# A two-layer recurrent kernel on one core: VectorE's weight work placed behind the first normalization, loads reordered, and a rearranged last block

## The chip, the cores and the metric

The kernel runs on one core of one Trainium2 chip. The core has five engines that run side by side, each with its own in-order queue: TensorE (PE in the profile, its weight loads PEld), VectorE (DVE), ScalarE (ACT), GpSimd (POOL) and SyncE (SP), which here only issues DMAs. The metric is device time of one execution in microseconds; lower is better.

## The reference

The input x has 4 sequences of 1024 tokens with 128 features. Two layers run over it. Each computes `x = x + s * g`, with xn the normalized x, s a sequence mixer and g the SiLU of a feed-forward network.

```python
x = L0_attn_x
xn = _layernorm(x)
s = _L0_attn_ref(xn, ...)        # q k^T with decay GAMMA**(i-j), times v
g = _silu(_L0_ffn_ref(xn, ...))  # silu(xn w1)*(xn w2), gelu(h1), gelu(h2), w3; width 512
x = x + s * g
xn = _layernorm(x)
s = _L1_attn_ref(xn, ...)        # W_in, causal conv of 4 taps, SiLU, state scan, SiLU gate, W_out
g = _silu(_L1_ffn_ref(xn, ...))  # top half of the tokens by router score through W1, GELU, W2
x = x + s * g
```

The state scan of the second layer keeps 16 states for each of the 128 features: `h = A*h + x_conv*B`, with `A = exp(-exp(A_log))`, and `y = sum(C*h) + D_param*x_conv`. The router takes the 512 highest of 1024 scores in each sequence.

## The kernel before

The 4096 tokens are cut into 8 blocks of 512 (NBK, HB); blocks 2b and 2b+1 are the halves of sequence b. Features lie on the 128 partitions, the 512 tokens of a block along the free dimension; x itself lies with tokens on partitions, in 4 chunks of 128 (CB).

**The order of the work** is not that of the text. Every helper (mm, act, copy, vcopy, vtt, stt, ptt, dma) only records an operation with an engine and an estimated cost. `Plan.order` then plays all recorded operations through a list scheduler: an operation has a due time (prio), an operation with an earlier due time goes first among those that are ready, and its ready time follows from the estimated costs, a model of the DMA ring, the free buffers of each pool tag, and 1.28 us for a change of ScalarE's table. That charge is made for SiLU, GELU and the tanh GELU only: `act` passes no table kind for Exp. `Plan.issue` emits the operations in that order (L373), each engine's order fixed by hand-made dependencies, so L373 is the line of nearly every instruction in the profile. Due times come from `TIMES`: for each stage a length and eight starts, one for each block, spread over the stage's operations by `Plan.spread`. An operation's `late` set holds others that must be planned before it without a semaphore between them.

**Start** (L508 to L649). All loads go on SP: x of block 0, vec, one table of constants cs (ident, mask, tie, sel, rowdec, coldec), wqk, A_log, the weights w12, wv, h1, h2 (in four row chunks each), w3 and so on, and x of blocks 1 to 4. VectorE rounds weights to the fp32r type by copies (w12_t, h_t, wgh, ...), some split in a high and a low part (M, wg, wcv, W1, wr). ScalarE computes logA by two Exp activations; VectorE copies it and tie into a PSUM bank, bankA. rep, four 128x128 selections of ident, is copied by VectorE too.

**Per block j**: `ln0` and `ln1` normalize by `layernorm`: bn_stats and bn_aggr on VectorE, ve = variance + eps (VectorE), rs = ve to the power -0.5 (GpSimd), tm = -mean*rs (VectorE), xn = x*rs + tm (ScalarE), four transposes tr (TensorE), then copies xh, xl. `retention` is the first mixer (pq, pv, psc, pz, po). `gated`, `hidden1`, `hidden2`, `out0` are the first feed-forward network: p and a; pa, ga, g_h and g_l; pb and h; pg. The parts g_h come from ScalarE, g_l from GpSimd. `front` is the convolution (px, xc) and stores xc to DRAM as xd. `states` makes B and C, `gates` the gate (pt), `router` the scores (pr), `moe` the second feed-forward network (pm, hm, pmo, ff), `ranks` the ranking (cmp, eq, rank, wm), `scans` the state scan, `project` W_out (y, pyo, so), and `finish` the gating and the store.

`scans` works through 8 tiles u of 128x2x512: DMA xd into u (broadcast to 16 states), u*B (VectorE), two scans along time (VectorE), u*C (GpSimd; the very last on VectorE), then sums over states into py (TensorE). There are 6 u buffers. In the last block the first two u tiles come from TensorE through rep (pu) instead of a DMA (U_BY_PE).

Of the kernel before, what the change touches and what calls it, by code (L numbers as in the profile page):

```python
# [8 lines left out]
FR = mybir.dt.float32r  # L9
# [4 lines left out]
P = 128  # L14
NB, L, D = 4, 1024, 128
NCH = L // P
HB = 512
# [30 lines left out]
for _name, _w in (  # L48
    ("ident", P), ("mask", P), ("tie", P), ("sel", P), ("rowdec", 1), ("coldec", 1),
):  # L50
    _CST[_name] = (_n, _n + _w)
    _n += _w
NCST = _n
# [7 lines left out]
    "ln0": (10.465, (-34.463, 37.568, 0.307, -8.702, 29.140, 25.837, -0.706, 2.276)),  # L61
    "retention": (7.697, (19.747, 29.540, 0.054, 5.261, 0.588, -0.481, 27.669, 17.510)),
    "gated": (0.198, (17.080, -12.778, -2.899, 37.127, 52.075, 3.684, 35.848, 24.681)),
    "hidden1": (181979.521, (10.669, -0.997, 0.654, 26.140, 49.753, 13.692, 29.323, 21.440)),
    "hidden2": (104.604, (6.706, 7.824, 35.607, 17.363, 7.255, 8.335, 12.787, 23.305)),
    "out0": (0.269, (-10.144, 10.621, 13.685, 32.888, 37.354, 6.208, 14.587, 34.725)),
    "ln1": (0.086, (-3.447, -9.822, 3.389, 39.108, 24.646, 10.527, 7.924, 19.641)),
    "front": (99775.310, (31.104, -7.375, 49.241, 35.721, 3.625, 15.911, 8.435, 28.268)),
    "states": (1929558528.870, (-22.925, -12.719, -2.927, -2.692, -1.385, 5.843, 8.364, 33.960)),
    "gates": (2802.502, (-10.124, -3.354, -1.683, 3.017, 7.752, 67.130, 11.212, 9.313)),  # L70
    "router": (35.459, (32.003, 36.047, 1.039, 23.096, 29.397, 12.314, 55.205, 9.245)),
    "moe": (0.850, (-6.037, 10.367, -2.942, 3.023, 8.714, 12.982, 45.904, 32.432)),
    "ranks": (3.658, (7.924, -5.386, 32.363, 0.750, 18.387, 5.771, 15.184, 9.739)),
    "scans": (0.083, (26.879, 6.452, 3.058, 25.041, 26.277, 9.568, 13.774, 14.948)),
    "project": (0.218, (-2.585, 1.221, 6.521, 8.046, 9.527, 12.283, 10.650, 21.658)),
    "finish": (2311.973, (10.042, -1.800, 14.285, 18.479, 29.156, 18.433, 18.474, 24.699)),
    "load_x": (0.107, (32.705, -1.570, 6.609, 55.729, 2.835, 7.712, 33.265, 51.716)),
}
SWITCH = 0.725
SPARE = 2  # L80
XB = 5
# [300 lines left out]
def tile_kernel(  # L382
# [34 lines left out]
    for name, n in {  # L417
        "x": XB, "stat0": 2, "ve0": 2, "rs0": 2, "tm0": 2, "stat1": 2, "ve1": 2, "rs1": 2, "tm1": 2, "col": 2, "wm": 2, "most": 2, "eq": 2,
        "nxt": 2, "xn0": 2, "xnT": 1, "qT": 1, "vd": 1, "sT": 1, "st": 1, "y": 1,
        "sc": 1, "xh0": 2, "xl0": 2, "sO": 2, "xh1": 2, "xl1": 2, "Br": 1, "Cr": 2, "bc": 1,  # L420
        "gate": 2, "xc": 2, "cmp": 2, "a": 3, "xn1": 3, "ff": 3, "so": 3,
        "hh": 8, "hl": 8, "h2": 5, "u": 6, "last": 2,
    }.items():
        early = name in ("a", "h2")
        plan.tag(sb, name, n, early or name in ("hh", "hl", "u"), 1 if early else None)
# [17 lines left out]
    def mm(o, lhsT, rhs, start, stop):  # L443
        n = rhs.length()
        one = rhs.root.dtype != F32
        cost = (n + 38) / 2400 if one else 4 * max(n / 2400, 0.0536)
        if o.shape[0] < P:
            cost += 0.12
        do("tensor", "matmul", o, lhsT=lhsT, rhs=rhs, start=start, stop=stop, cost=cost)
# [62 lines left out]
    cs = load("cs", cst, (P, NCST))  # L512
    wqk_s = load("wqk_s", wqkT, (P, 2 * D), "sT")

# [3 lines left out]
    wv_t = load("wv_t", wv, (P, D))  # L518
    sel = load("sel", by_state(cst[:, slice(*_CST["sel"])]), (P, P))
# [28 lines left out]
    def c(name):  # L548
        a, b = _CST[name]
        return cs[:, a:b]  # L550
# [5 lines left out]
    ident = c("ident")  # L556
# [34 lines left out]
    w12_t = tile_("const", "w12_t", (P, 2 * F), FR)  # L591
# [3 lines left out]
    for i, s in enumerate(h_s):  # L595
        h_t.append([tile_("const", f"h{i}_t{k}", (P, F), FR) for k in range(KC)])
        for k in range(KC):
            vcopy(h_t[i][k], s[k])
# [6 lines left out]

    rep_t = tile_("const", "rep", (P, 4 * P))
    rep = [rep_t[:, i * P : (i + 1) * P] for i in range(4)]
    for i in range(4):
        vcopy(rep[i].split(NS), c("ident")[:, 4 * i * E : (4 * i + 1) * E].repeat(NS))
    vcopy(A, logA)  # L610
    vcopy(tie, c("tie"))
# [30 lines left out]
    def add_bias(dst, i):  # L642

        mm(dst, two, bias[:, i * D : (i + 1) * D].repeat(CB), False, True)
# [4 lines left out]
    wr = split(wr_s, "wr", (P, P))  # L649

    def layernorm(j, u, tag):
# [14 lines left out]
        stt(tm, mv[:, :, 0], -1.0, rs, ALU.mult, ALU.mult)  # L666
        xn = tile_(tag, f"xn_{u}", (P, CB, D))
# [144 lines left out]
    def front(j):  # L812

        b, g = divmod(j, NH)
        px = mm_tile(f"px_{j}")
        terms = []
        for k in range(4):
            hi, lo = (t[:, k : k + HB] for t in R[j]["parts"])
            terms += three_pass(wcv, (hi, lo), slice(k * D, (k + 1) * D))
        passes(px, terms)  # L820
        if not g:
            vtt(px[:, 0:3], px[:, 0:3], edges, ALU.subtract)
        xc, xd = tile_("xc", f"xc_{j}"), tile_("xd", f"xd_{j}")
        act(AF.Silu, xc, px, bias=cbias)
        dma(xd, xc)
        R[j].update(xc=xc, xd=xd)

    def states(j):
        xc = R[j]["xc"]
        if j in BY_PE:  # L830
            Bp, Cr = tile_("B", f"B_{j}"), tile_("Cr", f"Cr_{j}")
            mm(Bp, wB, xc, True, True)
            if j in U_BY_PE:
                R[j]["Br"] = Br = tile_("Br", f"Br_{j}")
                act(AF.Identity, Br, Bp, bias=bB)
            act(AF.Identity, Bp, Bp, bias=bB)
# [84 lines left out]
    def scans(j):  # L921
# [7 lines left out]
        for m in range(4):  # L929
            us = []  # L930
            for q in range(0, 4, 2):
                ks = [4 * q + m, 4 * (q + 1) + m]
                u = tile_("u", f"u_{j}_{ks[0]}", (P, 2, HB))
                if m == 0 and j in U_BY_PE:
                    for i, k in enumerate(ks):
                        pu = mm_tile(f"pu_{j}_{k}")
                        mm(pu, rep[q + i], xc, True, True)
                        vtt(u[:, i, :], pu, R[j]["Br"], ALU.mult)
                else:
                    for i, k in enumerate(ks):  # L940
                        dma(u[:, i, :], xd[k * E : (k + 1) * E, :].whole(NS), 0.63, 2.24e5)
                    vtt(u, u, Bp.repeat(2), ALU.mult)
# [15 lines left out]
    def project(j):  # L958
        py = R[j]["py"]
        y = tile_("y", f"y_{j}")  # L960
        stt(py, R[j]["xc"], v("Dp"), py, ALU.mult, ALU.add)
        vtt(y, py, R[j]["gate"], ALU.mult)
        po = mm_tile(f"pyo_{j}", (P, CB, D))
        with fused("tensor", 1.15):
            for i, t in enumerate(chunk):
                mm(po[:, i, :], y[:, t], wout_t, i == 0, False)
            add_bias(po, 0)
        R[j]["so"] = so = tile_("so", f"so_{j}", (P, CB, D))
        copy(so.flat(), po.flat())

    def finish(j):
# [7 lines left out]
        tt = vtt if j == NBK - 1 else ptt  # L979
        tt(so, so, ff, ALU.mult)  # L980
        tt(xg, xg, so, ALU.add)
        dma(out[b, g * HB : (g + 1) * HB, :].rearrange("(c p) d -> p c d", p=P), xg)
# [6 lines left out]
    for j in range(NBK):  # L989
        b, g = divmod(j, NH)  # L990
        for f in (ln0, retention, gated, hidden1, hidden2, out0, ln1, front, states, gates, router, moe, scans, project):
            stage(f, j, j)
        if g == NH - 1:
# [93 lines left out]
```

## Time and profile before

| | |
|---|---|
| median of 3 runs | 418.02 us (417.58 to 420.35) |
| the profiled execution, all | 417.93 us |
| its span, first to last instruction | 416.2 us |
| granted TensorE clock, mean | 0.978 |
| instructions | 6589 |
| ScalarE table loads | 39, 1283 ns each, 50.0 us |
| u multiplied by C on GpSimd | 63, 2389 ns each, 149.7 us |
| u multiplied by B on VectorE | 62, 1206 ns each, 73.5 us |
| scans on VectorE | 128, 1207 and 1266 ns each, 153.3 us |
| loads of u | 124 DMAs of 256 KB, 4.6 us from issue to landing |

Times inside the execution count from the start of the span. A row of the profile in order of time gives start, busy time, engine, line, operation, output <- input with shapes, and in brackets how long the engine had been idle before and what ended that. Busy times of neighbouring rows can overlap a little, since an instruction starts before the one in front has written its last element; the distance from start to start is what a queue pays.

### The profile page before, as it was taken

What the parts mean: (1) busy time and instruction counts of PE and PEld (TensorE: products, weight loads), DVE (VectorE), ACT (ScalarE), POOL (GpSimd) and SP (SyncE); (2) the same over time, 40 slices, a digit from 0 to 9 for tenths busy, and PEclk for the clock granted to TensorE, in tenths of its full rate; (3) what the DMA queues carried; (4) which work ended last, traced back from release to release, by engine and by line L of the source; (5) the groups of instructions that cost most, each with busy time, mean ns of one, the idle gap of its engine ahead of it and who ended that gap; (6) DMA issues with size and microseconds to landing.
All of it is one profiled execution on the core that took longest, in us unless ns stands there. A gap on an engine that the chain in (4) does not pass through costs nothing.

```text
span 416.2 us, 6589 instructions
## 1 busy us (share of the span) xinstructions
PE 389.7 (94%) x2294; PEld 291.1 (70%) x2294; DVE 354.4 (85%) x621; ACT 276.3 (66%) x487; POOL 288.1 (69%) x200
## 2 busy tenths in 40 slices
PE   1999999999999999999999999999999999989843
PEld 1878878866777778777687688677877687747501
DVE  5594605996999968989999969999999999999992
ACT  3687895876557857875867598668577656772600
POOL 3066542198486897869996488967788898773890
PEclk9999999999999999999999999999999999998966
DMA  6900009206418053573602490456073553517300
GB/s 214 330 30 1 2 25 248 57 10 156 120 51 255 27 158 102 133 199 105 202 3 54 132 252 2 116 165 160 1 228 101 158 127 104 125 56 198 103 25 25
DMA packets 37897, 47.44 MB, mean 114 GB/s; under 512 B 7844, under 2 KB 17700, under 8 KB 37864
## 3 DMA queue, kind: packets, MB, share of 16 engines
q1 hardware_dynamic: 37864, 47.02, 40.8%
q8 instruction: 18, 0.29, 0.3%
q14 instruction: 15, 0.12, 0.1%
HBM read 42.40 MB, written 4.60 MB: 113 GB/s over the span
## 4 chain that ended last, share of the span: by engine, by line
PE 82%; DVE 5%; ACT 5%; POOL 4%; issue 2%; DMA 1%; POOLq 1%; SPq 1%; DVEq 0%; ACTq 0%
PE pb L373 15%; PE pa L373 12%; PE p L373 7%; PE py L373 7%; PE pg L373 6%; PE px L373 5%; PE pmo L373 5%; PE pm L373 4%; DVE u L373 4%; PE po L373 3%; POOL u L373 3%; PE pyo L373 2%; PE pv L373 2%; PE psc L373 2%; PE tr L373 2%
## 5 line engine op out<-in xcount | busy, mean ns | idle before, releaser
L373 POOL TENSOR_TENSOR u<-u,Cr 128x1024 f32<-128x1024 f32 x63 | 149.7, 2389 | 31.1 <-ACT last L373 13.0
L373 DVE TENSOR_TENSOR u<-u,B 128x1024 f32<-128x1024 f32 x62 | 73.5, 1206 | 17.1 <-DMA u<-xd 8.7
L373 DVE TENSOR_TENSOR_SCAN u<-bankA,last,u 128x512 f32<-128x512 f32 x64 | 78.5, 1266 | 0.2
L373 DVE TENSOR_TENSOR_SCAN u<-bankA,u 128x512 f32<-128x512 f32 x64 | 74.8, 1207 | 0.4
L373 POOL TENSOR_TENSOR h_l<-a,h_h 128x512 fp32r<-128x512 f32 x32 | 40.9, 1293 | 26.6 <-ACT h_h L373 26.6
L373 ACT ACT_TABLE_LOAD x39 | 50.0, 1283 | 13.6 <-PE pg L373 5.8
L373 POOL TENSOR_TENSOR g_l<-ga,g_h 128x512 fp32r<-128x512 f32 x32 | 40.6, 1293 | 20.5 <-ACT g_h L373 20.5
L373 PE MATMUL pa<-h_h,h_t 128*128 128x512 f32 x128 | 49.6, 405 | 0.0
L373 PE MATMUL pa<-h_l,h_t 128*128 128x512 f32 x128 | 48.6, 397 | 0.0
L373 PE MATMUL pb<-g_h,h_t 128*128 128x512 f32 x128 | 47.3, 396 | 0.0
L373 PE MATMUL pb<-g_l,h_t 128*128 128x512 f32 x128 | 47.1, 395 | 0.1
L373 PE MATMUL py<-u,sel 128*32 128x512 f32 x256 | 40.0, 633 | 7.2 <-POOL u L373 7.2
L373 ACT ACTIVATE h<-pb,vec 128x512 f32<-128x512 f32 x32 | 20.6, 688 | 18.1 <-PE pb L373 16.4
L373 PEld LDWEIGHTS pmo<-W_t,hm 128*128 128x128 f32 x256 | 31.1, 192 | 1.9 <-ACT ff L373 0.8
L373 PE MATMUL pmo<-W_t,hm 128*128 128x128 f32 x256 | 31.5, 275 | 0.0
L373 PEld LDWEIGHTS pg<-w_t,h 128*128 128x128 f32 x256 | 29.9, 192 | 1.0 <-ACT h L373 0.3
L373 PE MATMUL pg<-w_t,h 128*128 128x128 f32 x256 | 30.1, 275 | 0.1
L373 ACT ACTIVATE xn<-x,tm,rs 128x128 f32<-128x128 f32 x64 | 26.9, 486 | 4.6 <-DVE tm L373 4.6
L373 PEld LDWEIGHTS pa<-h_h,h_t 128*128 128x128 f32 x128 | 23.9, 188 | 7.5 <-issue 1.1
L373 PEld LDWEIGHTS pb<-g_h,h_t 128*128 128x128 f32 x128 | 23.9, 188 | 7.0 <-ACT g_h L373 1.3
L373 PEld LDWEIGHTS pa<-h_l,h_t 128*128 128x128 f32 x128 | 24.1, 188 | 6.4 <-POOL u L373 0.8
L373 PEld LDWEIGHTS pb<-g_l,h_t 128*128 128x128 f32 x128 | 23.9, 188 | 6.6 <-POOL g_l L373 1.4
(170 smaller groups left out, 838.3 us busy)
## 6 DMA issues: line engine op xcount, KB each, us to landing
u<-xd SPq DMA_DIRECT2D x124, 256.0 KB, 4.6
x<-in_x_dram SPq DMA_DIRECT2D x8, 256.0 KB, 2.9
xd<-xc SPq DMA_DIRECT2D x8, 256.0 KB, 2.0
out_dram<-x SPq DMA_DIRECT2D x8, 256.0 KB, 3.6
Br<-bd SPq DMA_DIRECT2D x6, 256.0 KB, 4.3
Cr<-bd SPq DMA_DIRECT2D x6, 256.0 KB, 5.6
h_s<-in_h1T_dram SPq DMA_DIRECT2D x4, 256.0 KB, 5.5
h_s<-in_h2T_dram SPq DMA_DIRECT2D x4, 256.0 KB, 4.2
```

Source lines behind the costliest of these rows:

```text
L373: i = getattr(getattr(self.nc, eng), method)(*map(real, args), **{k: real(a) for k, a in kw.items()})
```

## The change

- `layernorm`: when the first one (block 0) has recorded tm, all VectorE operations on weights recorded between `setup = len(plan.ops)` and the definition of `layernorm` get tm in their `late` set, so they are planned behind it. The copies of logA and tie into bankA are recorded after block 0's `ln0`, due at 0.5.
- Loads: ident has a tile and a load of its own, straight after wqk; cs is only mask, rowdec and coldec, and comes behind wv; tie is loaded by itself into the bc buffer. TIMES holds new values, and `mm`'s cost for fp32r is 44 instead of 38 columns over its length.
- `LAST_U`: in the last block the u tiles at index 2 (of 8) take the buffer of w12_t and those at 3 to 6 the four buffers of the hidden weights h_t, which are now laid out in pairs of row chunks (tags w12 and hw); the others take u buffers.
- rep is made in `states` of the last block, by four ScalarE copies into the xnT buffer.
- `project` and `finish` of the last block work in two halves of 256 tokens: py, y, the product with W_out and the last multiplication and addition, and two stores. so*ff reads the product from PSUM, without ScalarE's copy. In all blocks the bias product goes first into pyo instead of last.
- In `front`, the tiles xc and xd are created earlier in the text.

```diff
-    ("ident", P), ("mask", P), ("tie", P), ("sel", P), ("rowdec", 1), ("coldec", 1),
+    ("ident", P), ("mask", P), ("rowdec", 1), ("coldec", 1), ("tie", P), ("sel", P),
...
-NCST = _n
+NCST = _CST["tie"][0]
...
+LAST_U = ("u", "u", "w12", "hw", "hw", "hw", "hw", "u")
...
-        "hh": 8, "hl": 8, "h2": 5, "u": 6, "last": 2,
+        "hh": 8, "hl": 8, "h2": 5, "u": 6, "last": 2, "w12": 1, "hw": 4,
...
-        cost = (n + 38) / 2400 if one else 4 * max(n / 2400, 0.0536)
+        cost = (n + 44) / 2400 if one else 4 * max(n / 2400, 0.0536)
...
-    cs = load("cs", cst, (P, NCST))
     wqk_s = load("wqk_s", wqkT, (P, 2 * D), "sT")
+    ident = load("ident", cst[:, slice(*_CST["ident"])], (P, P))
...
     wv_t = load("wv_t", wv, (P, D))
+    cs = load("cs", cst[:, P:NCST], (P, NCST - P))
+    tie_s = load("tie_s", cst[:, slice(*_CST["tie"])], (P, P), "bc")
...
+    setup = len(plan.ops)
-    w12_t = tile_("const", "w12_t", (P, 2 * F), FR)
+    w12_t = tile_("w12", "w12_t", (P, 2 * F), FR)
...
-        h_t.append([tile_("const", f"h{i}_t{k}", (P, F), FR) for k in range(KC)])
+        pairs = [tile_("hw", f"h{i}_t{k}", (P, 2, F), FR) for k in range(KC // 2)]
+        h_t.append([pairs[k // 2][:, k % 2, :] for k in range(KC)])
...
-    for i in range(4):
-        vcopy(rep[i].split(NS), c("ident")[:, 4 * i * E : (4 * i + 1) * E].repeat(NS))
-    vcopy(A, logA)
-    vcopy(tie, c("tie"))
...
+    setup = [o for o in plan.ops[setup:] if o.eng == "vector"]
...
         stt(tm, mv[:, :, 0], -1.0, rs, ALU.mult, ALU.mult)
+        for o in setup:
+            o.late.add(plan.ops[-1])
+        setup.clear()
...
+                rep = tile_("xnT", "rep", (P, 4, P))
+                R[j]["rep"] = rep = [rep[:, i, :] for i in range(4)]
+                for i in range(4):
+                    copy(rep[i].split(NS), ident[:, 4 * i * E : (4 * i + 1) * E].repeat(NS))
...
-                u = tile_("u", f"u_{j}_{ks[0]}", (P, 2, HB))
+                home = LAST_U[2 * m + q // 2] if j == NBK - 1 else "u"
+                u = tile_(home, f"u_{j}_{ks[0]}", (P, 2, HB))
...
+        n = CB // 2 if j == NBK - 1 else CB
+        R[j]["po"] = po = [mm_tile(f"pyo_{j}_{h}", (P, n, D)) for h in range(0, CB, n)]
+        for h, p in zip(range(0, CB, n), po):
+            t = slice(h * P, (h + n) * P)
+            stt(py[:, t], R[j]["xc"][:, t], v("Dp"), py[:, t], ALU.mult, ALU.add)
+            vtt(y[:, t], py[:, t], R[j]["gate"][:, t], ALU.mult)
+            with fused("tensor", 0.23 * (n + 1)):
+                add_bias(p, 0, True)
+                for i in range(n):
+                    mm(p[:, i, :], y[:, chunk[h + i]], wout_t, False, i == n - 1)
...
+            for h in range(0, CB, CB // 2):
+                t = slice(h, h + CB // 2)
+                vtt(so[:, t, :], R[j]["po"][2 * h // CB], ff[:, t, :], ALU.mult)
+                vtt(xg[:, t, :], xg[:, t, :], so[:, t, :], ALU.add)
+                dma(to[:, t, :], xg[:, t, :])
...
+            if j == 0 and f is ln0:
+                place(0.5)
+                vcopy(A, logA)
+                vcopy(tie, tie_s)
```

## The prediction

> **What bounds the kernel now.** First the busy shares and the 40 slices: which engine is full, and where.
>
> ```profile
> PE 389.7 (94%) x2294; PEld 291.1 (70%) x2294; DVE 354.4 (85%) x621; ACT 276.3 (66%) x487; POOL 288.1 (69%) x200
> ...
> PE   1999999999999999999999999999999999989843
> ...
> DVE  5594605996999968989999969999999999999992
> ```
>
> TensorE is full in every slice but the first and the last ones; nearly all of its 26.5 us of idle time lies at the two ends. The table of equal stretches (columns: length, TensorE, its weight loads, VectorE, ScalarE, GpSimd, clock, DMA) says the same. Most rows give TensorE 25.8 to 26.00 of 26; the ends do not:
>
> ```profile
> 0.00:26.00 26.00, 16.72 (x80) 13.47 (x81) 16.51 (x68) 14.44 (x26) 9.46 (x19) 1.00 0.73 229
> ...
> 364.00:390.00 26.00, 24.42 (x154) 16.18 (x151) 25.17 (x45) 16.38 (x27) 14.18 (x9) 0.93 0.40 103
> 390.00:416.00 26.00, 12.00 (x47) 3.43 (x45) 18.57 (x18) 3.22 (x8) 14.72 (x8) 0.71 0.22 61
> ```
>
> So a gain at the head moves all that follows, a stall put into the middle is paid in full, and the end belongs to VectorE. TensorE's waits between 26 and 366 us are 0.68, 0.23 and 0.19: 1.1 us in all.
>
> Head, in order of time: block 0's normalization is ve (VectorE), rs (GpSimd), tm (VectorE), xn (ScalarE).
>
> ```profile
> 6.55 0.35 DVE L373 TENSOR_SCALAR wqk<-wqk_s,th 128x256 f32<-128x256 f32 x1 [0.41 <-DMA wqk_s<-in_wqkT_dram]
> 6.82 0.15 DVE L373 TENSOR_SCALAR ve<-bankA 128x4 f32<-128x4 f32 x1
> ...
> 8.66 0.15 DVE L373 SCALAR_TENSOR_TENSOR tm<-bankA,rs 128x4 f32<-128x4 f32 x1
> ...
> 8.85 1.65 ACT L373 ACTIVATE xn<-x,tm,rs 128x128 f32<-128x128 f32 x4 [2.89 <-DVE tm L373]
> ```
>
> ve stands behind wqk, whose load was issued fifth, at 3.02; tm comes half a microsecond after rs ended (8.16), behind weight work.
>
> ScalarE in block 0's hidden layers, the place that I count on most below:
>
> ```profile
> 26.69 1.28 ACT L373 ACT_TABLE_LOAD   x1 [1.04 <-PE pa L373]
> 27.98 1.27 ACT L373 ACTIVATE ga<-pa,vec 128x512 f32<-128x512 f32 x2
> ...
> 30.17 0.70 ACT L373 ACTIVATE ga<-pa,vec 128x512 f32<-128x512 f32 x1
> 30.91 0.59 ACT L373 CAST xh<-tr 128x512 fp32r<-128x512 f32 x1
> 31.39 0.62 ACT L373 CAST g_h<-ga 128x512 fp32r<-128x512 f32 x1
> 31.91 0.70 ACT L373 ACTIVATE ga<-pa,vec 128x512 f32<-128x512 f32 x1
> ...
> 35.63 1.85 ACT L373 ACTIVATE h<-pb,vec 128x512 f32<-128x512 f32 x3 [2.03 <-PE pb L373]
> ```
>
> The first h (36.2) is ready only 1.7 us before TensorE wants it: pg starts at 37.93 and ends at 41.42.
>
> The end:
>
> ```profile
> 404.62 1.23 DVE L373 TENSOR_TENSOR u<-u,Cr 128x1024 f32<-128x1024 f32 x1
> 407.87 0.75 DVE L373 SCALAR_TENSOR_TENSOR py<-xc,vec,py 128x512 f32<-128x512 f32 x1 [2.03 <-PE py L373]
> 408.65 0.69 DVE L373 TENSOR_TENSOR y<-py,gate 128x512 f32<-128x512 f32 x1
> 411.45 0.69 DVE L373 TENSOR_TENSOR so<-so,ff 128x512 f32<-128x512 f32 x1 [2.10 <-ACT so L373]
> 412.18 0.69 DVE L373 TENSOR_TENSOR x<-x,so 128x512 f32<-128x512 f32 x1
> ```
>
> From 383.5 to 405.8 VectorE has no gap: it waits for no u transfer there.
>
> The sum is made in this execution's own times: 416.2 us of span, 417.93 us in all, 1.7 us outside the span; the median of the runs, 418.02, is 0.1 higher.
>
> **1. Head.** In the built queue of the changed kernel SP issues x, vec, wqk_s, ident, w12_s. Issues are about 0.5 us apart, so vec goes at 1.22, in A_log's old slot, and wqk at 1.70. A_log (issued 1.22, used at 4.13) took 2.9 us, wqk took 3.5: vec lands near 4.1, wqk at 4.6 to 5.2. VectorE: statistics from 3.58 (0.79), th at about 4.6, ScalarE's exp 0.2 to 5.0, four aggregations of 0.16, wqk 5.2 to 5.55, last aggregation, ve at 5.7. Then 0.15 for ve, 0.16 to GpSimd, 1.03 for rs, 0.13 back: tm at 7.1 with only Mh and Ml in front, against 8.66: **-1.55** (bounds -0.9, if wqk lands 0.6 later than the slower row, and -1.9). The weight work now held behind tm (w12, edge, wr, two, h1) is some 3.5 us before xl at 11.2; xl was at 12.18, so it gains only 1.0, but its first reader stood 1.4 us after its end (12.87 to 14.29), which covers the missing half. The casts themselves are as many; VectorE then idled 3.37 us at 16.90, which takes the rest. cs lands behind wv, needed only by vd (14.67). sel, bB, bC, wout go last and are used from 60 us on. ident by itself adds one issue, tie one more, about 0.5 us each on SP, whose 29 loads ended near 18 us; the next SP work waits for xc, after 60 us. The four rep copies (0.13 from start to start) leave VectorE and become four ScalarE copies in block 7's xnT, between xn and xh; ScalarE's small copies take 0.2 and a 128x128 one 0.41, so 0.8 to 1.6 us, on an engine 66% busy: zero, or at most 1.6 if xh stands behind them.
>
> **2. A's two exponentials.** A_log's load is now 26th on SP, and both exponentials of logA move out of the head, where they shared the one table load at 0.72 with th's. In the built ScalarE queue they stand after ga_2 and after g_3, inside block 0's Gelu work, and each has a table load before it and one after it: four new ones (a fifth is elsewhere; 44 against 39). This is the edit that speaks against the change. In before's time, without the head's shift: ga_2 ends 30.85; load to 32.14; exponential 0.22; xh to 32.9 (was 31.4); g_2 to 33.4 (31.9); load to 34.7; ga_3 to 35.3; xnT 35.8; g_3 to 36.3 (33.5); load to 37.6; exponential to 37.8. Here VectorE is caught too: the copy of logA into bankA is queued in front of ve_4 and tm_2, so tm_2 comes at 38.3, and xn_2, the next on ScalarE, from 38.5 to 40.1; load to 41.4; first h at 42.05. TensorE meets this as 0.7, 0.4 and 1.3 us of waiting in pb (for g_2_h, g_2_l, g_3_h) and then at pg, which starts at 42.1 instead of 37.93: **+4.2**. What stood behind (W1, bias, wgl on VectorE; rs_3 on GpSimd) is first needed after 47 us. Bounds: +3.5 if xn_2 finds tm_2 early (xn_2 at 37.8), +4.5 if the loads carry gaps like the 0.02 us at 351.21; below +3.5 only if ScalarE's queue ran otherwise than built. From 41.42 on TensorE had no idle time up to 88 us, so nothing gives it back.
>
> The row's load is 1.28 us and the Gelu behind it starts 0.01 us later. The Trainium skill, "ScalarE: Activation LUTs", under "What ACT_TABLE_LOAD costs", counts a drain of about 1.38 us on top of the load, 2.66 us for each switch. This trace shows no such gap. By the page, four switches would be 5.5 us dearer and the time near 425.
>
> **3. New start times and queue order (TIMES, mm's cost).** The order within the middle changes, the work does not. Summing TensorE's rows up to the last px gives the same in both queues. Taken at 0; bounds -1.1 (every wait of the middle gone) and +4 (the slower rival).
>
> **4. Last block up to the scans.** TensorE's queue now has 5.6 us of work from tr_7 to the end of px_7 (was 6.95, 355.75 to 362.7), so block 7's xl on VectorE comes 1.35 us later, about 357.85 instead of 356.44, and the ranking instructions at 367.4 instead of 366.01. From there 38.6 us led to the last scan; 0.83 of it were waits on rank and pu (0.56 and 0.27), which go, since pu_0, pu_4 and pC now stand in front of the ranks. **+0.5**, bounds -0.8 and +1.4. The u tiles in the memory of w12 and of the hidden weights let u's loads start sooner, but no VectorE instruction of the end waited for one: 0. What limits u_1 to u_11 is VectorE's own 2 multiplications and 4 scans per round (2.3 + 4.7 us), three times.
>
> **5. Output in halves.** From py complete (407.87) to x written (412.87) took 5.0 us: two multiplications, four products with bias (1.39), a ScalarE copy (0.62), two more multiplications. Two 512-wide instructions follow each other at 0.6 to 0.7 us, so a half is 0.33 to 0.4. Both halves of py, then y: y's first half done near 408.95; two products without bias (issued before) 0.6; so and x of half 0 to 410.5; half 1, whose products lie beside that, to 411.35. **-1.5** with ScalarE's copy gone. The last store is half as large (before: 3.3 us from x to the end); bounds -1.0 and -2.0.
>
> Sum: -1.55 + 4.2 + 0 + 0.5 - 1.5 = +1.65; 417.93 + 1.65 = **419.6 us**.
>
> **Rivals.** *Faster:* the table loads fall into ScalarE's idle time. For it: ScalarE waited 2.03 us at 35.63 and 1.04 at 26.69. Against: the loads stand in its queue in front of g_2, g_3 and h, and 5.1 + 0.4 us do not fit into 2.7. Were they free, with the waits of part 4 gone: -1.55 - 0.8 - 1.5 = -3.85, 414.1; with the middle's 1.1 as well, 413.0. *Slower:* the second normalization becomes the bound in the middle. In block 3 only 10.0 us of TensorE work (py 3.0, pm 2.8, pt 0.7, pmo 3.5) now lie between the end of pg and tr, where it was some 14; in block 7 about 10, as before, when the chain took 10.4 (343.85 to 354.29) with xn waiting for other ScalarE work. One u-by-Cr row of GpSimd (2.36 us) in front of rs in both makes TensorE wait 2 us twice: +1.65 + 4 = 423.6. It decides from the point where that chain exceeds 10 us. *The change does not do what it says:* true for the u memory, already counted as 0.
>
> **How the numbers follow.** About 1% (4.2 us) is what a measurement of this kernel tells from no change. Forecast 0.5: 417.5 to 422, likeliest 419.6. Faster rival 0.25, 411.5 to 417, a little over half of it under 413.8. Slower rival 0.25, 422 to 427. So faster by over 1%: 0.17; within: 0.56 (nearly all of the forecast and the rest of the faster case); slower: 0.27. Leaving out one in ten at each end gives 413 to 425.
>
> **What would show it.** Four table loads of 1.28 us between 25 and 42 us; TensorE idle about 4 us there, with pg of block 0 starting near 40.5 (42.1 less the head's 1.55). xn of block 0 near 7.3. VectorE without gaps after 383 us again. Two last stores, x done about 3.5 us before the end of the span. The forecast falls if pg starts before 38.5, or if TensorE's waits between 45 us and the last px add up to more than 3.

## The result, and the profile after

The changed kernel takes 421.74 us (median of 6 runs, 421.54 to 424.06); the kernel before takes 418.15 us beside it. The ratio is 1.009, 95% interval 1.0066 to 1.0115: 0.9% slower. The profiled execution has a span of 419.9 us against 416.2, so +3.7 us have to be found, where the forecast had +1.65.

Shares and slices on the page of the changed kernel (the first line gives busy microseconds; a digit below is the busy tenth of one of 40 equal slices):

```profile
PE 394.3 (94%) x2295; PEld 292.5 (70%) x2295; DVE 355.3 (85%) x621; ACT 282.1 (67%) x495; POOL 287.4 (68%) x200
...
PE   3997999999999999999999999999999999989943
...
DVE  5783514799999974989998989999999997999995
```

The same stretches of 26 us as before, with one more (length, TensorE, its weight loads, VectorE, ScalarE, GpSimd, clock, DMA):

```profile
0.00:26.00 26.00, 18.73 (x88) 14.99 (x89) 17.80 (x74) 15.22 (x25) 9.44 (x19) 1.00 0.76 227
26.00:52.00 26.00, 22.95 (x123) 17.80 (x121) 12.85 (x43) 22.89 (x37) 13.61 (x12) 1.00 0.00 0
364.00:390.00 26.00, 23.96 (x133) 15.43 (x132) 25.69 (x46) 13.73 (x24) 15.09 (x8) 0.87 0.51 142
390.00:416.00 26.00, 17.41 (x88) 8.21 (x86) 24.09 (x24) 8.57 (x17) 17.08 (x10) 0.87 0.04 11
```

The first stretch holds 2 us more of TensorE work (16.72 before): the head came forward. The second holds 3 us less than full: a stall that the kernel before did not have. The last one is fuller because everything in it lies later.

Block 0's normalization in the changed kernel, VectorE's rows in order of time (start, busy time, engine, line, operation):

```profile
4.79 0.35 DVE L374 TENSOR_SCALAR wqk<-wqk_s,th 128x256 f32<-128x256 f32 x1
...
5.27 0.16 DVE L374 TENSOR_SCALAR ve<-bankA 128x4 f32<-128x4 f32 x1
...
6.64 0.16 DVE L374 SCALAR_TENSOR_TENSOR tm<-bankA,rs 128x4 f32<-128x4 f32 x1
```

ScalarE's row there, in the bracket the time it stood idle before and what ended it:

```profile
6.84 1.65 ACT L374 ACTIVATE xn<-x,tm,rs 128x128 f32<-128x128 f32 x4 [2.23 <-DVE tm L374]
```

tm comes at 6.64 instead of 8.66; the first pq follows at 9.69 instead of 11.71.

ScalarE in block 0's hidden layers, changed kernel:

```profile
28.99 1.28 ACT L374 ACT_TABLE_LOAD   x1
30.28 0.22 ACT L374 ACTIVATE logA<-A_log 128x16 f32<-128x16 f32 x1
...
31.51 1.28 ACT L374 ACT_TABLE_LOAD   x1
32.80 0.69 ACT L374 ACTIVATE ga<-pa,vec 128x512 f32<-128x512 f32 x1
...
34.50 1.28 ACT L374 ACT_TABLE_LOAD   x1
35.80 0.22 ACT L374 ACTIVATE logA<-logA 128x16 f32<-128x16 f32 x1
36.64 1.65 ACT L374 ACTIVATE xn<-x,tm,rs 128x128 f32<-128x128 f32 x4 [0.63 <-issue]
38.31 1.28 ACT L374 ACT_TABLE_LOAD   x1
39.61 2.42 ACT L374 ACTIVATE h<-pb,vec 128x512 f32<-128x512 f32 x4
```

What TensorE meets there, in the changed kernel (its rows with idle time):

```profile
32.91 0.50 PE L374 MATMUL pb<-g_l,h_t 128*128 128x512 f32 x1 [0.17 <-POOL g_l L374]
34.54 0.50 PE L374 MATMUL pb<-g_h,h_t 128*128 128x512 f32 x1 [1.13 <-ACT g_h L374]
...
40.35 3.84 PE L374 MATMUL pg<-w_t,h 128*128 128x128 f32 x32 [1.58 <-ACT h L374]
```

Four loads of 1.28 us around two exponentials of 0.22 us: the second g_h and the h behind them are what TensorE waits for, and pg starts at 40.35 instead of 37.93 in spite of the earlier head.

The end of the changed kernel, VectorE's rows:

```profile
409.03 2.88 DVE L374 TENSOR_TENSOR u<-u,Cr 128x1024 f32<-128x1024 f32 x1
413.06 1.02 DVE L374 SCALAR_TENSOR_TENSOR py<-xc,vec,py 128x256 f32<-128x256 f32 x2 [1.16 <-PE py L374]
414.11 0.75 DVE L374 TENSOR_TENSOR y<-py,gate 128x256 f32<-128x256 f32 x2
415.41 0.42 DVE L374 TENSOR_TENSOR so<-pyo,ff 128x256 f32<-128x256 f32 x1 [0.54 <-PE pyo L374]
415.87 0.43 DVE L374 TENSOR_TENSOR x<-x,so 128x256 f32<-128x256 f32 x1
416.21 0.42 DVE L374 TENSOR_TENSOR so<-pyo,ff 128x256 f32<-128x256 f32 x1
416.66 0.42 DVE L374 TENSOR_TENSOR x<-x,so 128x256 f32<-128x256 f32 x1
```

GpSimd's last row beside them:

```profile
408.47 2.35 POOL L374 TENSOR_TENSOR u<-u,Cr 128x1024 f32<-128x1024 f32 x1
```

Behind a wait of 0.54 us for the first product the halves follow each other without a gap. New is the first row: VectorE's last u by Cr takes 2.88 us instead of 1.23, and GpSimd's last one lies beside it. In the kernel before, GpSimd's last one ended at 404.72, 0.1 us after VectorE's had begun at 404.62:

```profile
402.37 2.35 POOL L373 TENSOR_TENSOR u<-u,Cr 128x1024 f32<-128x1024 f32 x1
```

Cut at milestones, the two spans compare so (start of the first pq and pa, of block 0's pg; end of the last px, of the last scan, of the last x; microseconds; the columns add up to the span):

| kernel | to pq | to pa | to pg | to px end | to scans end | to x | to the end | span |
|---|---|---|---|---|---|---|---|---|
| before | 11.71 | 10.46 | 15.76 | 324.80 | 41.78 | 8.36 | 3.3 | 416.2 |
| changed | 9.69 | 10.45 | 20.21 | 326.04 | 42.54 | 8.16 | 2.8 | 419.9 |
| difference | -2.0 | 0 | +4.45 | +1.2 | +0.8 | -0.2 | -0.5 | +3.7 |

The experiments are read in the same columns, each from one profiled execution, since their medians also contain what differs from run to run (last section).

### The profile page after: what moved, and what is told of

Its sections match the earlier page's. It is cut to its first block, busy times and chain, and to the rows that moved or that the text cites. A ratio compares the mean times of both kernels' runs of the same rounds, so it can differ in the third digit from the quotient of the medians.

```text
span 419.9 us, 6593 instructions
## 1 busy us (share of the span) xinstructions
PE 394.3 (94%) x2295; PEld 292.5 (70%) x2295; DVE 355.3 (85%) x621; ACT 282.1 (67%) x495; POOL 287.4 (68%) x200
## 4 chain that ended last, share of the span: by engine, by line
PE 76%; ACT 6%; POOL 4%; DVE 4%; issue 2%; POOLq 0%; DVEq 0%; ACTq 0%
PE pb L374 14%; PE pa L374 13%; PE py L374 7%; PE pg L374 7%; PE pmo L374 6%; PE p L374 6%; PE px L374 4%; PE pm L374 4%; POOL u L374 3%; PE po L374 2%; PE pyo L374 2%; ACT L374 2%; DVE u L374 2%; PE pv L374 1%; PE pt L374 1%
## 5 line engine op out<-in xcount | busy, mean ns | idle before, releaser
L374 POOL TENSOR_TENSOR g_l<-ga,g_h 128x512 fp32r<-128x512 f32 x32 | 40.9, 1301 | 17.2 <-ACT g_h L374 17.1
L374 PE MATMUL pb<-g_h,h_t 128*128 128x512 f32 x128 | 49.0, 407 | 1.3 <-ACT g_h L374 1.1
L374 PE MATMUL pa<-h_h,h_t 128*128 128x512 f32 x128 | 48.7, 404 | 0.0
```

Source lines behind the costliest of these rows:

```text
L374: i = getattr(getattr(self.nc, eng), method)(*map(real, args), **{k: real(a) for k, a in kw.items()})
```

## The experiments

Theory: the four table loads cost what the prediction said (4.2), the halves give 1.5; the 2.1 us that it missed are two things that are not in the diff's text, the pace of TensorE's products in the middle (+1.2) and the meeting of VectorE and GpSimd at the last u by Cr. Rivals: the middle has slack, and the loads are not the cause; or the middle is longer by its new order. All experiments that move single instructions do it behind the planner, so that no other instruction changes its place in its queue (tiles can come to lie elsewhere, see "Where the tiles lie"):

```diff
+    def moved(self, ops):
+        out = list(ops)
+        ...
+        return out
-        for o in self.order():
+        for o in self.moved(self.order()):
```

`after(o, p)` in it takes o out of the list and puts it straight behind p.

| kernel | to pq | to pa | to pg | to px end | to scans end | to x | to the end | median, us |
|---|---|---|---|---|---|---|---|---|
| exponentials early | 10.57 | 10.19 | 16.28 | 326.04 | 42.55 | 8.16 | 2.8 | 418.26 |
| one pair of loads | 9.91 | 11.44 | 20.25 | 325.93 | 42.54 | 8.63 | 2.8 | 421.13 |
| copy of logA behind tm | 9.85 | 10.62 | 19.48 | 326.08 | 42.55 | 7.86 | 2.9 | 421.43 |
| before, four loads added | 11.60 | 11.41 | 18.51 | 324.70 | 43.30 | 8.36 | 3.3 | 421.73 |
| sum x + so on VectorE | 10.34 | 11.61 | 20.16 | 326.09 | 42.54 | 8.08 | 2.8 | 422.88 |
| both, early and sum | 10.60 | 11.29 | 16.28 | 326.02 | 42.55 | 6.52 | 2.8 | 417.67 |
| tiles shifted | 10.54 | 10.66 | 20.18 | 324.56 | 42.56 | 8.57 | 2.8 | 421.83 |
| u in its own buffers | 10.08 | 11.31 | 20.21 | 326.11 | 42.55 | 7.85 | 2.9 | 422.47 |
| before, halves alone | 11.72 | 10.30 | 15.75 | 324.80 | 41.49 | 7.38 | 2.7 | 415.89 |
| all three mendings | 9.77 | 11.28 | 16.16 | 324.45 | 42.57 | 6.80 | 2.8 | 415.01 |
| old order, new head | 9.84 | 11.10 | 19.38 | 325.78 | 41.80 | 7.22 | 2.8 | 419.77 |
| before, new start times | 11.22 | 11.35 | 17.07 | 333.13 | 41.06 | 9.46 | 3.3 | 428.89 |

The kernel before ran beside each of them, at 418.06 to 418.66 us.

**The exponentials early.**

```diff
+        wv = find("sync", "wv_t")
+        after(find("sync", "A_log"), wv)
+        x = find("scalar", "xnT_0")
+        e1, e2 = find("scalar", "logA"), find("scalar", "logA", 1)
+        after(e2, x)
+        after(e1, x)
```

> The changed kernel with every queue as it was, but for five instructions: A_log's load goes behind wv_t's on SP (7th), and both exponentials of logA go behind ScalarE's copy xnT of block 0, where the exponential's table is still loaded. So the four table loads of block 0's Gelu work are gone, and nothing else. Theory (the loads delay g_l, g_h, the second block's xn and h, and TensorE pays 4.4 us that nothing gives back): first product pg back from 40.35 to 36.0 (up to 36.4 if the two exponentials of 0.2 us delay vd), time 421.74 - 4.4 = 417.3 (417.0 to 417.8). Rival A (the middle has slack after all, the delay is made up there): 420.5 or more although pg starts near 36. Rival B (the 1.1 us that TensorE's middle lost beyond pg are also due to the stall): 416.2.

TensorE's row of pg in this run, now without a wait in front of it:

```profile
37.04 3.73 PE L404 MATMUL pg<-w_t,h 128*128 128x128 f32 x32
```

From pa to pg 16.28 us instead of 20.21: the loads cost 3.9 us, and the stretches after pg keep their lengths, so nothing is made up later (rival A falls) and the middle is as long as with the stall (326.04; rival B falls). The median fell by 3.5, not 4.4: the profiled execution reached pq 0.9 later, on a later load of wqk.

**One pair of loads.**

```diff
+        e1, e2 = find("scalar", "logA"), find("scalar", "logA", 1)
+        after(e2, e1)
```

> The changed kernel, but the second exponential of logA directly behind the first on ScalarE: one pair of table loads stays (before and after the first two exponentials), the pair around 35 to 39 us goes. Theory (cost depends on where a load stands: the first pair holds g_l and g_h in front of pb, 2.8 us in all, the second pair holds only h in front of pg): pg starts when pb ends, at 38.8 instead of 40.35, so -1.6, 420.1 (419.8 to 420.4). Rival A (each load costs the same 1.1 us): -2.2, 419.5. Rival B (the second pair lies beside TensorE's pb and costs nothing): 421.7.

A miss in this profile: pa to pg stayed at 20.25. The run's stretches of 2 us show why (columns as in the stretches above; the granted clock is the third number from the end):

```profile
34.00:36.00 2.00, 0.70 (x3) 0.21 (x2) 0.56 (x1) 1.92 (x4) 1.26 (x2) 1.00 0.00 0
36.00:38.00 2.00, 2.00 (x5) 1.61 (x6) 1.89 (x7) 1.36 (x4) 1.99 (x2) 0.53 0.00 0
38.00:40.00 2.00, 2.00 (x7) 1.52 (x7) 1.64 (x7) 0.29 (x1) 1.57 (x2) 0.61 0.00 0
```

The wait of 1.14 us for g_h is in the first of them (TensorE 0.70 busy of 2.00); straight after it the granted clock was a half for 3.4 us, which is 1.7 us of work at the full clock, about what the saved pair was to give. Four of the six runs lie at 419.72 to 421.40 (mean 420.7; 420.1 was expected), and two near 423.4, the profiled one among them. So the pair's own price is not settled by this profile, but a wait of TensorE has a second price here.

**The copy in front of tm.**

```diff
+        after(find("vector", "bankA", 0, "logA"), find("vector", "tm_0_2"))
```

> The changed kernel with one instruction moved: VectorE's copy of logA into bankA goes behind tm of the third normalization, in front of which it stood. The four table loads stay. Theory (the prediction's step: tm waits for the copy, the copy for the second exponential, so ScalarE idles 0.63 us in front of xn and h comes as much later): xn directly behind the exponential, the next table load 0.6 earlier, TensorE's wait at pg 1.58 - 0.6 = 0.95, so pa to pg 19.6 us instead of 20.2, time -0.6, 421.1. Rival (xn waits for rs of GpSimd, not for the copy): pa to pg 20.2, time 421.7.

TensorE's row of pg in this run:

```profile
39.95 3.84 PE L399 MATMUL pg<-w_t,h 128*128 128x128 f32 x32 [0.85 <-ACT h L399]
```

As expected: xn follows the exponential at once, the wait in front of pg fell from 1.58 to 0.85, pa to pg 19.48, -0.73. The median alone (421.43) lies between theory and rival. VectorE's queue carried a part of the loads' delay to ScalarE.

**The loads alone, in the kernel before.** Two exponentials whose results nobody reads are added.

```diff
+    dum = tile_("const", "dum", (P, NSC))
+    act(AF.Exp, dum, A_log)
+    act(AF.Exp, dum, dum, scale=-1.0)
+    ...
+        e1, e2 = find("scalar", "dum"), find("scalar", "dum", 1)
+        after(e1, find("scalar", "ga_0_2"))
+        after(e2, find("scalar", "g_0_3_h"))
```

> The kernel before with two more exponentials of 16 values, whose results nobody uses, on ScalarE where the changed kernel has logA's: behind ga_2 and behind g_3 of block 0. Four more table loads, nothing else moves, and no VectorE copy waits for them. Theory (what a load delays is the work queued behind it; here the second normalization's xn stands behind three h, so h is held only by the loads): g_2 and g_3 late as in the changed kernel, pb's waits 0.2 and 1.1, its end 2.8 later, pg at 40.7 against 37.93: +2.8, 421.0 (420.6 to 421.6). Rival (ScalarE's idle 2.0 us in front of h takes the loads): pg by at most 1.0 later, 419.3 or less.

Two of TensorE's rows in this run, the last wait in pb and pg:

```profile
37.28 0.50 PE L400 MATMUL pb<-g_h,h_t 128*128 128x512 f32 x1 [1.12 <-ACT g_h L400]
41.52 3.73 PE L400 MATMUL pg<-w_t,h 128*128 128x128 f32 x32
```

From pa to pg 18.51 against 15.76: +2.75, the +2.8 expected. With three h in front of xn TensorE no longer waits in front of pg; the changed kernel's 3.9 is this plus what xn and the copy add in front of h. The median, 421.73, is a little above the range told. The profiled execution also lost 1.5 us from px to the end of the scans: its clock was a half from 375.8 to 382.6 us, over the ranking, and VectorE waited 2.2 us for rank products there (0.8 in the kernel before).

**VectorE and GpSimd at the last u by Cr.**

```diff
+        x = find("gpsimd", "x_6", 1)
+        x.eng, x.calls = "vector", [("vector", *k[1:]) for k in x.calls]
+        after(x, find("vector", "u_7_11", -1))
+        ...
```

> The changed kernel, but the last-but-one block's sum x + so goes from GpSimd (where it stands in front of the last u by Cr) to VectorE, behind its own last u by Cr, where VectorE waits 1.16 us for py. All else in the same order. Theory (VectorE's last u by Cr took 2.88 us instead of 1.23 because GpSimd's u by Cr ran beside it): GpSimd's ends 1.2 us earlier, near 409.6, VectorE's u by Cr takes 1.6 to 1.9 us, py is complete 1.0 us earlier, time -1.0 (-0.7 to -1.3), 420.7. Rival (VectorE's long u by Cr has another cause, such as a wait for u or Cr that the row hides): it takes 2.9 us still, time 421.7 or, with 0.7 us of new work on VectorE, 422.4.

The row of VectorE in this run:

```profile
410.85 1.22 DVE L404 TENSOR_TENSOR u<-u,Cr 128x1024 f32<-128x1024 f32 x1
```

GpSimd's last row in this run:

```profile
408.47 2.34 POOL L404 TENSOR_TENSOR u<-u,Cr 128x1024 f32<-128x1024 f32 x1 [0.46 <-DVE u L404]
```

The mechanism is shown: GpSimd ends at 410.81, VectorE's instruction starts then and takes 1.22 us. In the other executions it took 2.88 us where GpSimd's lay beside its first 1.79 us, 1.71 to 1.77 us where it lay beside 0.6 to 0.7, 1.51 us where it lay beside 0.43, and it ended 1.08 to 1.09 us after GpSimd's end each time. So VectorE does next to nothing while GpSimd holds on. How far GpSimd's lay over it, 0.6 to 1.8 us, differed between executions with the same order there; why, no run shows. The Trainium skill, "SBUF — State Buffer", section "SBUF: two separate sides", says it as a rule: the ports that the two share are an exclusive lock, held for a whole instruction, and the other blocks. These rows agree.

But the time did not fall (422.88). To x it took 8.08 us against 8.16: the 1.66 us saved were spent on TensorE's clock. Two stretches of 2 us around the last products, first of the changed kernel:

```profile
404.00:406.00 2.00, 0.95 (x4) 0.19 (x4) 2.00 (x3) 0.00 (x0) 2.00 (x2) 0.50 0.00 0
...
412.00:414.00 2.00, 1.33 (x5) 0.29 (x5) 0.90 (x2) 0.00 (x0) 0.00 (x0) 1.00 0.00 0
```

The same two stretches of this run:

```profile
404.00:406.00 2.00, 0.23 (x2) 0.19 (x4) 2.00 (x3) 0.00 (x0) 2.00 (x2) 0.87 0.00 0
412.00:414.00 2.00, 2.00 (x7) 0.21 (x5) 0.67 (x2) 0.00 (x0) 0.00 (x0) 0.50 0.18 51
```

At 412 the changed kernel has the full clock (1.00) and this run the half one (0.50): here the half clock began at 405.5 instead of 402.4 us and lasted to the end instead of to 409.3. From VectorE's u by Cr to py complete it is then 2.0 us instead of 1.1, and from py to x 4.8 us instead of 4.1. Over all profiled executions it is 1.1 us to py where the clock was full there (four of them) and 1.9 to 2.0 where it was a half for all or most of it. The profiled execution was also 1.8 us longer up to pa (pq 0.65 later, 11.61 us from pq to pa); whether that holds for the other runs, and so for the 1.1 us by which the median is higher, is not shown.

**Both, exponentials early and the sum on VectorE.**

> The changed kernel with both edits: exponentials early (as in the run with no table loads) and the sum x + so of the last-but-one block on VectorE. Theory (both are paid in full and do not meet): 421.74 - 4.4 - 1.0 = 416.3 (415.8 to 417.0), below the kernel before by 1.8. Rival (what is saved early is lost again in front of VectorE's end, as VectorE is full from 383 us on): no lower than 418.

Together with the early exponentials the clock was full from 405.1 to 415.4 us: 6.52 us to x, -1.64 against the changed kernel, and 417.67 us in all, 0.15% below the kernel before (interval of the ratio 0.9970 to 0.9999). That it is 1.4 more than expected goes with the start of the profiled execution: pq 0.9 later, and 0.8 more from pq to pa. Against the exponentials early alone the median fell by 0.6 us, so the 1.64 are one execution's, clock included.

**Where the tiles lie.** Two tiles are made longer; the instructions and their order are those of the changed kernel.

```diff
-        for name, i in (("bB", 0), ("bC", NS))
+        for name, i, n in (("bB", 0, 1), ("bC", NS, 88))
...
-    A, logA = bankA[:, 0:NSC], tile_("const", "logA", (P, NSC))
+    A, logA = bankA[:, 0:NSC], tile_("const", "logA", (P, 64))[:, 0:NSC]
```

> The changed kernel, same instructions in the same order; two small tiles are made longer (bC by 320 bytes, logA by 192 bytes per partition), so that the halves of the hidden activations that TensorE streams (hh, hl) begin at a multiple of 128 bytes, as the hidden weights do, and both at the same place within 512 bytes. Theory: the 1.1 us that the middle lost beyond pg is a matter of where the operands lie. Before, both began at multiples of 128 bytes and pb's matmuls followed each other every 228 ns; in the changed kernel (weights at a multiple, streamed halves 64 bytes past one) and with the exponentials early (the other way round) every 233 ns. So pa and pb go from 233 to 228 or 229 ns; 512 of them make -2.0 to -2.5, time 419.5. Rival (the pace comes from the new order of the matmuls or from the run): 233 ns as before, time 421.7.

Four products of pb in a row in the changed kernel, TensorE's rows (the distance from start to start is what counts):

```profile
30.13 0.40 PE L374 MATMUL pb<-g_l,h_t 128*128 128x512 f32 x1
30.37 0.39 PE L374 MATMUL pb<-g_h,h_t 128*128 128x512 f32 x1
30.60 0.40 PE L374 MATMUL pb<-g_l,h_t 128*128 128x512 f32 x1
30.84 0.39 PE L374 MATMUL pb<-g_h,h_t 128*128 128x512 f32 x1
```

Four of them with the tiles shifted:

```profile
31.41 0.40 PE L374 MATMUL pb<-g_h,h_t 128*128 128x512 f32 x1
31.64 0.39 PE L374 MATMUL pb<-g_l,h_t 128*128 128x512 f32 x1
31.88 0.39 PE L374 MATMUL pb<-g_h,h_t 128*128 128x512 f32 x1
32.10 0.39 PE L374 MATMUL pb<-g_l,h_t 128*128 128x512 f32 x1
```

0.71 us for three steps there, 0.69 here. The difference is seen better in the mean over all starts less than 0.3 us apart between 45 and 375 us:

| kernel | begin of weights, of streamed halves, modulo 512 bytes | pa, ns | pb, ns | pg to last px, us |
|---|---|---|---|---|
| before | h0 352 and 384, h1 384; 384 | 231.5 | 228.6 | 324.80 |
| changed | 128; 320 | 233.3 | 233.4 | 326.04 |
| exponentials early | 192; 384 | 233.1 | 233.4 | 326.04 |
| before, new start times | h0 320 and 352, h1 384; 384 | 231.4 | 228.9 | |
| tiles shifted | 128; 128 | 229.1 | 228.8 | 324.56 |
| all three mendings | 192; 192 | 229.9 | 228.8 | 324.45 |

The middle is back at 324.56 us with not one instruction changed: the +1.2 is the place of the tiles, and the rival, the new order of the products, falls. Added up by product from pg to the last px, pa and pb took 1.76 us more in the changed kernel than in the kernel before, and 1.70 of these went with the shift; the others moved by 0.1 in all. Modulo 512 bytes the shift moved only the streamed halves and ten other kinds of tiles, among them ff and some weights of the second layer. The median stayed at 421.83, since this execution came to pq 0.85 later and had the half clock at the end.

> The changed kernel with all three mendings: exponentials early, the sum x + so of the last-but-one block on VectorE, and bC longer by 320 bytes. Here hidden weights and streamed halves both begin 64 bytes past a multiple of 128, but at the same place within 512 bytes. Theory (the place of the two relative to each other sets the pace): pa and pb at 228 to 229 ns, from pg to the last px 324.5 us instead of 326.0, time 417.7 - 1.5 = 416.2. Rival (each must begin at a multiple of 128 bytes): 233 ns, 326.0 us, time 417.7.

Here both begin 64 bytes past a multiple of 128 and the pace is as good, so it is the two's place relative to each other that goes with the pace, not each by itself. For pb this is shown at two distances, 0 and 192 bytes; what makes it so is not. pa is less clean (231 ns in the kernel before for the three chunks of h0 that lie at the same place, too). At 415.01 us, ratio 0.9915 to the kernel before (0.9892 to 0.9938), this has the lowest median of the study; its interval overlaps with that of the halves alone (below).

**The order alone: a miss.** The kernel before with the new TIMES and mm's new cost:

```diff
...
-        cost = (n + 38) / 2400 if one else 4 * max(n / 2400, 0.0536)
+        cost = (n + 44) / 2400 if one else 4 * max(n / 2400, 0.0536)
```

> The kernel before with only the new start times and the new cost of a matmul: the new order of the middle and of the end, without the late exponentials, without weight work held back, without halves. Theory (the new order costs the end: ranks later, GpSimd's last u by Cr beside VectorE's): last px as before or up to 0.6 earlier, ranking instructions 1.2 later against px, VectorE's last u by Cr near 2.9 us, so +1 to +2, 419.2 to 420.2. Rival (the order is free, and the extra 1.9 us of the changed kernel's middle and end came with the late exponentials and the placement of its tiles): 418.3. In this build h1's weights and the streamed halves begin at the same place within 512 bytes, h0's do not: if placement sets the pace, pb has 228 ns and pa 233 here.

428.89 us, 10 slower: TensorE waited 11.4 us for GpSimd's u in py (7.2 in both kernels of the comparison), and its clock was a half from 396 us to the end. The planner made an order that is neither kernel's from these numbers, so the run says nothing on the changed kernel's order (of the placement, pb came out as expected, pa between the two paces); it shows that start times fitted to one program don't carry to another.

**u in its own buffers.**

```diff
-LAST_U = ("u", "u", "w12", "hw", "hw", "hw", "hw", "u")
+LAST_U = ("u",) * 8
```

> The changed kernel with the last block's u tiles all in their own six buffers, as in the kernel before (w12's and the hidden weights' memory stays unused after them); on SP one store moves in front of five of the loads. Theory (the memory of u does nothing): VectorE has no gap for a u transfer between the ranking instructions and the last scan, 38.1 to 38.5 us from the first ranking instruction to the end of the scans, time 421.7 within what runs differ. Rival (the loads into dead memory were needed in the new order): VectorE waits for u, +1 or more, 422.7.

From px to the end of the scans 42.55 us as with the dead weights' memory (42.54). That part of the change does nothing; in the profiled execution the start was longer (1.2 us more up to pa), which may be the 0.7 us of the median.

**The halves alone.** project and finish of the changed kernel in the kernel before.

```diff
+        n = CB // 2 if j == NBK - 1 else CB
+        R[j]["po"] = po = [mm_tile(f"pyo_{j}_{h}", (P, n, D)) for h in range(0, CB, n)]
+        ...
+                vtt(so[:, t, :], R[j]["po"][2 * h // CB], ff[:, t, :], ALU.mult)
+                vtt(xg[:, t, :], xg[:, t, :], so[:, t, :], ALU.add)
+                dma(to[:, t, :], xg[:, t, :])
```

> The kernel before with the output in halves alone (last block's products, bias first, sums and store in two halves, no ScalarE copy). Theory (prediction's term): -1.5, 416.8 (416.3 to 417.2). Rival (part of the 1.5 seen in the changed kernel came from TensorE's granted clock, which was full there from py on and halved before for py): py to x written 4.7 to 5.0 instead of 4.0, last store 0.5 shorter, -0.8, 417.5.

VectorE's first and last row of the end:

```profile
407.42 1.01 DVE L373 SCALAR_TENSOR_TENSOR py<-xc,vec,py 128x256 f32<-128x256 f32 x2 [2.02 <-PE py L373]
...
411.02 0.43 DVE L373 TENSOR_TENSOR x<-x,so 128x256 f32<-128x256 f32 x1
```

From py complete to x 4.07 us instead of 5.05 with the clock full over the four products in both, and the last store 0.5 less: -1.5 in the profile, and the theory holds. The medians differ by 2.8 (415.89 us, ratio 0.9931, 0.9905 to 0.9956). This profiled execution also gained 0.3 from px to the scans and 0.2 from pq to pa, and the kernel before ran 0.7 above its own profiled execution there; no more of the difference is accounted for.

**The old order with the new head.** The changed kernel with the old TIMES, exponentials early, and tiles at matching places.

```diff
+        after(find("sync", "ident"), find("sync", "wqk_s"))
...
-        cost = (n + 44) / 2400 if one else 4 * max(n / 2400, 0.0536)
+        cost = (n + 38) / 2400 if one else 4 * max(n / 2400, 0.0536)
```

> The parts that paid, put together: the changed kernel's code with the old start times and the old cost of a matmul (so the order of the middle and of the end is almost the one of before), A_log's load and both exponentials early, ident's load behind wqk's, and two small tiles (th, bC) made longer so that hidden weights and streamed halves begin at multiples of 128 bytes and at the same place within 512. Theory (terms add): before with halves alone gave 415.9; new head -2.0 (wqk near 4.8, tm near 6.7), pa's matmuls 229 instead of 231.5 ns -0.4: 413.5 (412.8 to 414.5). Rival (the head's gain does not reach the end, because TensorE starts at its slow pace and VectorE's last stretch waits for something else): 415.3 or more.

419.77 us, a failure: the head was there (pq at 9.84), but the new plan let TensorE wait 2.0 us in block 0's pb, with a half clock behind it (31.9 to 35.4 us), and 0.8 us for g again in a later pb. It has one use: with the old order the stretch from px to the end of the scans is 41.80 us, with the new one 42.55. The new order costs the end 0.75 us there. In the other executions with the old order it is 41.49, 41.78 and, with the half clock over the ranking, 43.30; in the nine with the new order 42.54 to 42.57.

## Why the prediction held, and where it was off

421.7 us lies within 413 to 425 and within 1% of before, 2.1 above the 419.6 of the sum. By its parts:

1. **Head**, -1.55: -2.0 in the profile; over all profiled executions with this head pq came at 9.7 to 10.6 against 11.2 to 11.7, on the mean 1.4 earlier. wqk's load is the spread. Of the 2.0 us, 1.55 lie in front of ve (5.27 against 6.82, behind wqk) and 0.47 between ve and tm (1.37 us against 1.84, the weight work); no run makes the one change without the other.
2. **A's two exponentials**, +4.2: 3.9 by undoing them, 4.45 between the two profiles. The other 0.5 stays with the exponentials early (16.28 against 15.76) and lies in pa's and pb's products. The order of events came as told, with waits of 0.17 and 1.13 us at pb (0.7, 0.4 and 1.3 told), 1.58 at pg, and pg at 40.35 (40.55 told). TensorE's idle time was 2.9 us, not about 4; the other 1.0 of the 3.9 lies in pb's products, which followed each other at longer distances beside the waits. The copy in front of tm, counted in, was worth 0.7. The faster rival, with the loads in ScalarE's idle time, is refuted. In the changed kernel, too, the activation behind a load starts 0.01 to 0.02 us after it; the drain that the Trainium skill, "ScalarE: Activation LUTs", section "What ACT_TABLE_LOAD costs", counts on top does not show, and the estimate by it, 425, was too high.
3. **Middle**, 0, bounds -1.1 and +4: +1.2. This is the step that failed: "The order within the middle changes, the work does not." True of the instructions, and the waits did shrink, from 1.2 to 0.5 us. But the step took each product's duration as given, and pa's and pb's changed by 2 and 5 ns through the place of tiles that the diff moves without naming them (448 products between pg and the last px, +1.76 in all; the waits -0.7, all else +0.2). The slower rival, with the second normalization, is refuted: TensorE waits 0.5 us in all between 45 us and the last px.
4. **Last block up to the scans**, +0.5: +0.8, and the run with the old order shows 0.75 of it. The first ranking instruction came 1.1 us later against px (1.4 told), and the stretch behind it shrank by 0.4 instead of 0.8: of its waits, 0.83 us in two, both for rank products, 0.31 stayed. The u memory: 0, as told.
5. **Halves**, -1.5: -1.5, shown alone. That the size agrees is in part luck: the step found 1.5 us between py complete and x (5.0 to 3.5) and nothing in the last store, and the run gave 1.0 there (5.05 to 4.07) and 0.5 in the store. Scans to x, where the 1.0 lies, gained only 0.2, since the step did not look at who else is busy there: GpSimd's late u by Cr added 1.65 us to VectorE's, and a full instead of half clock for py gave 0.87 back. These two belong to this execution: in four others with the same end (one pair of loads, copy of logA behind tm, tiles shifted, u in its own buffers) VectorE's row grew by 0.5 only and py came at the half clock, as before. The end loses 0.5 to 0.8 us by the two together.

So -2.0 + 4.45 + 1.2 + 0.8 - 1.5 + 1.65 - 0.87 = +3.7.

## What to carry to other kernels

An instruction that a list planner may place freely should carry all that it costs: two exponentials of 0.2 us, priced without their table, cost 4 us. After a change, compare the distance from start to start of the commonest instruction and the place of its operands too, since a change that only shifts tiles can move the pace of all products. When a stretch gets shorter on one engine, look at who shares ports with it at the new time.

## What the hardware showed beyond expectation

- **Operand places.** 228.6 ns or 233.4 ns for one and the same product pb of 512 columns, with weights and streamed tile at the same place within 512 bytes or 192 bytes apart.
- **TensorE's clock comes in steps of 3.4 us.** In the clock records of all executions it changes between 1.0 and 0.5 after 3.41 us or multiples (6.8, 10.2, 17.1, 20.5). The Trainium skill, "TensorE: Matmul & The Clock Gate", section "What's actually happening", names such a window, 3413 ns, free-running, and gives the half clock after an idle window. The records agree on the length; a whole idle window was not needed here: in the 3.41 us ahead of the half clock at 36.13 us (one pair of loads) TensorE was busy for 1.84, and 1.83 us of work in a stretch of the changed kernel (37.21 to 40.62) was followed by the full clock. At the start the full clock came between 13.3 and 17.4 us of the span in kernels with the same first products, 2.9 to 6.0 us behind the first pq; from pq to pa that makes 10.2 to 11.6 us, later the later it came. Such a spread of 1.4 us is as large as most effects here, and it is why profiled executions are compared by stretches. The same product of block 0 in two runs, first TensorE's row with the exponentials early, whose record of the full clock begins at 13.5 us:

```profile
14.07 0.40 PE L404 MATMUL p<-xh,w_t 128*128 128x512 f32 x1
```

And with both mendings, where it begins at 16.0 us:

```profile
14.60 0.63 PE L410 MATMUL p<-xh,w_t 128*128 128x512 f32 x1
```

- **One stall, two prices.** A wait of little more than 1 us was followed by 3.4 us at half clock in some executions (36.1 to 39.5 us with one pair of loads), in others not. Where a later wait covered it, it cost nothing: with u in its own buffers the clock was a half from 36.0 to 39.5 us, the wait in front of pg was gone, and pa to pg took 20.21 us as in the changed kernel.
